# Graph convolution and masked attention on one core: small parameters loaded last, attention's first chunks reordered, the range check moved beside the last chunk

## The chip, the cores and the metric

The kernel runs on one core of a Trainium2 chip. The metric is the device time of one execution in microseconds (us), taken as the median of several runs; here it is 3640.62 us. The profile is of one execution, 3639.4 us from its first to its last instruction. Engines are named as the profile names them: PE is TensorE's matmul, PEld its weight load, DVE VectorE, ACT ScalarE, POOL GpSimd and SP SyncE, whose queue starts most transfers. A "q" behind a name (SPq, PEldq) is that engine's sequencer.

## What is computed

Two layers over x (8 batches of 2048 nodes with 256 features) and one adjacency matrix of 2048 x 2048, all in float32.

```python
# layer 0
A_norm = adj + eye;  dinv = rsqrt(rowsum(A_norm) + colsum(A_norm) - diag(A_norm))
agg = (A_norm * dinv[:, None] * dinv[None, :]) @ x            # for each batch
h = relu(batchnorm(agg @ W1.T + b1, g1, be1))                 # 512 wide
x = layernorm(x + batchnorm(h @ W2.T + b2, g2, be2))          # 256 wide
# layer 1: 4 heads of 64, mask where adj == 0
q, k, v = split(x @ W)
attn = softmax(q @ k.T / 8 + where(adj == 0, -inf, 0)) @ v
out = layernorm(x + attn)
```

The softmax is computed without subtracting the row's maximum. At the end a range check counts the row sums that lie outside 1e-20 to 1e30. If there is one, the whole attention is done again with maxima (`attention_with_maxima`, L1045); otherwise a branch jumps over that code.

## The kernel before, in words

**The load of the adjacency (L195 to L272).** Sixteen row tiles of 128 x 2048 (1 MB each, `a`, three buffers, L217) come in on SP's queue. For each tile PE makes sixteen transposes (L231, into PSUM tiles `ps`, four buffers), DVE and ACT copy them out (L237, L235), ACT sums the rows (L239), DVE takes the diagonal (L220), PE adds up the columns by a product with ones (L241, `pc`), and POOL prepares the mask's diagonal (L246, L247). The load of a further tile into a buffer waits until all of these have read it. In this block the order of SP, POOL and DVE is the order of the code; PE and ACT are ordered by the scheduler. Six small parameters are loaded at the very beginning, each with one transfer on SP's queue that scatters single floats to 128 partitions (L71): `b1s`, `g1s`, `be1s` (4 a partition) and `b2s`, `g2s`, `be2s` (2 a partition). They are first read by L366, by the first batch norm, by L557 and by the second batch norm. After the sixteenth tile come four loads of x (L251), the first weights (L252) and the writes of half of the transposed adjacency to DRAM, `bt_d`, four times 2 MB (L254).

**Layer 0 (L277 to L619).** Products of half-matrices on PE (`product`, L326: eight float32 matmuls of 512 columns into one of four PSUM tiles `pa`), with sums on DVE and POOL around them. Three difference tiles (`t2`, `t3`, `t4`) overwrite the quarters written out by L254, so each waits for one of these writes. The copy L390 waits for the last, because its tile lies in memory that the fourth quarter held.

**Attention's input and start (L989 to L1023).** The first batch has four chunks of 512 rows, numbered 0 to 3. For each chunk in turn: batch norm on ACT (`bn`), turned on PE and added to x on DVE in two halves (`turn_y`, `add_y`, through PSUM tile `st`), with the layer norm's statistics on DVE, and then its root on POOL (`root`). `ready(c)` applies the layer norm on ACT and, for chunks 0 and 1, turns the result on PE (`turn`, copied to `x1t` by ACT). `project` makes keys (1), queries (0) or values (2) of one chunk. The order here is written out by hand and kept on PE, DVE, ACT and POOL: all four chunks, `ready(0)`, three projections, `ready(1)`, the first scores.

**Attention (L1024 to L1043).** 64 units (batch, pair of heads, chunk of 512 queries), each of 16 steps, one for every 128 keys. A step computes scores on PE (L824), the mask on DVE (L836), the exponential on ACT (L842), the weighted sum of values on PE (L854) and the row-sum accumulator on POOL (L865). Scores run three steps ahead. Other work is hung onto steps by `at_step(unit, step, f)`; what is due after the last unit runs at the end, in order of its step. At the end of a unit: the sums are completed on PE (L881), copied by ACT (L889), turned on PE (L895), put into `sums_all` by DVE (L897); the outputs are turned (L908) and added to x (L916, 8 instructions, `finish` in two halves). For the second pair of heads follow the output's layer norm: `emit_stats` on DVE (L656, L658), `root` on POOL (L95, L97, L663, L664, four columns), `emit` on ACT (L668) and one 512 KB store on SP's queue (L749).

**The end (L1123 to L1141).** The range check runs after everything, in two pools of its own whose memory is reused: two instructions on DVE (L1130, L1131), one matmul (L1135), one conversion (L1136). Then each engine loads the count into a register (L1139) and branches (L1140).

Of the kernel before, what the change touches and what calls it, by code (L numbers as in the profile page):

```python
# [21 lines left out]
SUM_MIN = 1e-20  # L22
SUM_MAX = 1e30
# [3 lines left out]
def tile_gcn_then_masked_attention(  # L27
# [15 lines left out]
    nc = tc.nc  # L43
    ENG = mybir.EngineType
    PSUM = bass.MemoryType.PSUM
    P = 128
# [8 lines left out]
    CH = 512  # L55
    NCH = N // CH
# [9 lines left out]
    mhalf = cpool.tile([P, NT], F32, name="mhalf")  # L66
    nc.gpsimd.memset(mhalf, -0.5)

    def column_param(src, n, name):
        t = cpool.tile([P, n], F32, name=name)  # L70
        nc.sync.dma_start(t, src.rearrange("(c p) -> p c", p=P))  # L71
        return t

    b1s, g1s, be1s = (column_param(s, NH, n) for s, n in ((b1, "b1s"), (g1, "g1s"), (be1, "be1s")))
# [120 lines left out]
    with tc.tile_pool(name="bt7", bufs=1, side="right") as bp7, tc.tile_pool(  # L195
# [54 lines left out]
        for i, j in HALVES:  # L250
            S[0, i, j] = load_form(i, j, 0)  # L251
        nc.sync.dma_start(w1s, w1t.rearrange("(c p) f -> p c f", p=P))  # L252
        for s, ij in enumerate(HALVES):
            nc.sync.dma_start(bt_d[s], T[1, ij])  # L254
        cs = sp1.tile([P, CH], F32, name="cs")
# [385 lines left out]
    def rows(b, k, src, n=CH):  # L641
        return src[b, k * n : (k + 1) * n, :].rearrange("(t p) d -> p t d", p=P)

    class LayerNorm:
# [28 lines left out]
    class Layer1Input:  # L673
# [44 lines left out]
            self.ln[b, c].stats(tiles)  # L718

        def root(self, b, c):  # L720
            self.ln[b, c].root()

        def apply(self, b, c, half):
            self.ln[b, c].apply(range(IT * half, IT * (half + 1)))
# [16 lines left out]
        def emit_stats(self, b, c, half):  # L741
            if half == 0:
                self.ln[b, c] = LayerNorm(self.pool, self.x1[b, c])
            self.ln[b, c].stats(range(IT * half, IT * (half + 1)))

        def emit(self, b, c, half):
            self.apply(b, c, half)
# [43 lines left out]
                )  # L791

    IN_ORDER = {ENG.PE, ENG.DVE, ENG.Activation, ENG.Pool}

    def attention():


        with tc.tile_pool(
# [111 lines left out]
            def finish(u, half):  # L910
                b, hp, c = units[u]
                for i in range(IT * half, IT * (half + 1)):
                    t = inp.x1[b, c][:, i, :]
                    for h in range(2):
# [3 lines left out]
                            op0=ALU.mult, op1=ALU.add,  # L918
                        )

# [67 lines left out]

            with tc.manual_schedule(engines=IN_ORDER):  # L989
                for c in range(NCH):  # L990
                    inp.yt[0, c] = y0[c]
                    inp.x1[0, c] = ip.tile([P, TPC, D], F32, name="x1", bufs=NCH + 3)
                    for o in range(NO):
                        inp.bn(0, c, o)
                    pm = ps_s.tile([P, TPC, D], F32, name="st")
# [4 lines left out]
                    inp.root(0, c)  # L1000
                right.close()
# [4 lines left out]
                def ready(c):  # L1006
                    for half in range(2):
                        inp.apply(0, c, half)
                    if c < 2:
                        for half in range(2):  # L1010
                            inp.turn(0, c, half)

                ready(0)
                inp.project(0, 0, 0, 1, k_on_act=True)
                inp.project(0, 0, 0, 0)
                inp.project(0, 0, 0, 2)
                ready(1)
                for g in range(LEAD):
                    mask_scores(g, scores(g))
                    exps(g)  # L1020
                    if g == 1:
                        inp.project(0, 0, 1, 1)
                        ready(2)  # L1023
# [96 lines left out]
    attention()  # L1120


    with tc.tile_pool(name="range", bufs=1, space=PSUM) as ps_c, tc.tile_pool(  # L1123
        name="range_s", bufs=1
    ) as rp:
        flat = sums_all.rearrange("p u t h -> p (u t h)")
        ok = rp.tile([P, NU * TPC * 2], F32, name="ok")
        cnt = rp.tile([P, 1], F32, name="cnt")
        bad = cpool.tile([1, 1], mybir.dt.int32, name="bad")
        nc.vector.tensor_scalar(ok, flat, SUM_MIN, None, op0=ALU.is_ge)  # L1130
        nc.vector.scalar_tensor_tensor(  # L1131
            ok, flat, SUM_MAX, ok, op0=ALU.is_le, op1=ALU.mult, accum_out=cnt
        )
        pc = ps_c.tile([1, 1], F32, name="pc")
        nc.tensor.matmul(pc, cnt, ones[:, :1], start=True, stop=True)  # L1135
        nc.vector.tensor_scalar(  # L1136
            bad, pc, -1.0, float(P * NU * TPC * 2), op0=ALU.mult, op1=ALU.add
        )
        n_bad = nc.values_load(bad[0:1, 0:1])  # L1139
    with tc.If(n_bad > 0):  # L1140
        attention_with_maxima()  # L1141

# [42 lines left out]
```

## Time and profile before

| What | Value |
|---|---|
| Median of 3 runs | 3640.62 us (3638.4 to 3642.35) |
| Span of the profile | 3639.4 us, granted PE clock 0.993 |
| PE, POOL, DVE, ACT busy | 99%, 76%, 55%, 45% |
| Chain that ended last | PE 96%, POOL 1%, DVE 1%, ACT 1% |
| First PE instruction | 9.18 us |
| Layer 0's last product to the first scores | 1247.29 to 1282.19 us |
| Last value product (L854) to the end | about 3614.9 to 3639.4 us |

Busy shares are an average over very different stages. The kernel is PE's nearly everywhere; what PE does not fill are the head (before the first tile lands), the passage from layer 0 to attention, and the tail after the last value product. There the chain of waits and the timeline tell more than the shares do.

### The profile page before, as it was taken

The page shows a single profiled execution, that of the slowest core. Times are in us where ns is not written, and L with a number is a line of the kernel's source. Part 1 is how long each engine was busy: PE and PEld are TensorE (multiplying, and loading weights), DVE is VectorE, ACT ScalarE, POOL GpSimd, SP SyncE. Part 2 cuts the span into 40 slices and gives each one's busy share as a digit, 9 for nine tenths or more (in the row PEclk, how much of TensorE's full clock was granted, in tenths as well). Part 3 has the DMA queues.
Part 4 walks back from the last instruction along what each step waited for, and adds up shares of the span by engine and source line. Part 5 has one row for each costly group of instructions (what it writes and reads, how often), then busy time and mean ns, then how long its engine had stood idle before and what let it go on. Part 6 is the DMA issues. An engine that isn't in the chain of part 4 may idle for free.

```text
span 3639.4 us, 55807 instructions
## 1 busy us (share of the span) xinstructions
PE 3587.3 (99%) x23055; PEld 1487.6 (41%) x23055; DVE 1989.5 (55%) x2929; ACT 1642.6 (45%) x2036; POOL 2757.1 (76%) x1457
## 2 busy tenths in 40 slices
PE   8999999999999899999999999999999999999997
PEld 4444444444444443433343433343433334343332
DVE  6212141221146646766766766676676676676665
ACT  5001100110135455655665665565566566556554
POOL 3443263424247678999999999999999999999996
PEclk9999999999999899999999999999999999999998
DMA  9122232230256300000010010010001000000000
GB/s 338 61 75 87 81 133 81 75 98 29 81 204 252 147 1 7 24 30 13 19 42 13 13 36 24 13 36 24 7 30 36 7 24 30 13 19 24 7 1 25
DMA packets 132761, 205.82 MB, mean 57 GB/s; under 512 B 6912, under 2 KB 113936, under 8 KB 122000
## 3 DMA queue, kind: packets, MB, share of 16 engines
q1 hardware_dynamic: 132032, 196.11, 15.6%
q0 software_dynamic: 288, 4.98, 0.4%
q8 instruction: 183, 3.00, 0.3%
q10 hardware_dynamic: 176, 1.06, 0.1%
q14 instruction: 82, 0.67, 0.1%
HBM read 126.62 MB, written 75.51 MB: 56 GB/s over the span
## 4 chain that ended last, share of the span: by engine, by line
PE 96%; POOL 1%; DVE 1%; ACT 1%; DMA 0%; issue 0%; SPq 0%; POOLq 0%; DVEq 0%; ACTq 0%
PE out_ps L854 25%; PE st L824 24%; PE pa L329 21%; PE pm L765 6%; PE ph L362 5%; PE pa L539 5%; PE pm L779 3%; PE pm L881 2%; PE pm L707 1%; PE pm L733 1%; PE ps L231 1%; PE pm L908 1%; PE pm L895 1%; POOL acc L865 1%; PE ph L584 1%; PE pc L241 0%
## 5 line engine op out<-in xcount | busy, mean ns | idle before, releaser
L865 POOL TENSOR_TENSOR acc<-acc,prob 128x1024 f32<-128x1024 f32 x823 | 1947.5, 2366 | 97.8 <-ACT prob L842 40.6
L836 DVE SCALAR_TENSOR_TENSOR prob<-mask,st 128x1024 f32<-128x1024 uint8 x1024 | 1243.3, 1219 | 616.9 <-PE st L824 582.0
L842 ACT ACTIVATE prob<-prob 128x1024 f32<-128x1024 f32 x1024 | 1082.3, 1057 | 945.4 <-DVE prob L836 925.1
L854 PE MATMUL out_ps<-prob,v 64*64 64x512 f32 x8192 | 1077.1, 596 | 1.7 <-DVE ot L870 1.7
L824 PE MATMUL st<-qt,kt 64*64 64x512 f32 x8192 | 1064.2, 590 | 0.1
L329 PE MATMUL pa<-t,x 128*128 128x512 f32 x1792 | 773.2, 594 | 2.7 <-ACT x L305 2.7
L824 PEld LDWEIGHTS st<-qt,kt 64*64 64x64 f32 x8192 | 312.8, 133 | 566.9 <-issue 528.3
L329 PEld LDWEIGHTS pa<-t,x 128*128 128x128 f32 x1792 | 341.3, 191 | 432.6 <-issue 428.4
L854 PEld LDWEIGHTS out_ps<-prob,v 64*64 64x64 f32 x8192 | 284.9, 132 | 511.6 <-issue 412.7
L410 POOL TENSOR_TENSOR ag<-ag,dbc 128x512 f32<-128x512 f32 x16 | 20.2, 1262 | 486.1 <-DVE ag L409 456.6
L366 ACT ACTIVATE h<-ph,b1s 128x512 f32<-128x512 f32 x112 | 77.0, 688 | 404.4 <-PE ph L362 404.4
L765 PE MATMUL pm<-x1t,wq 128*128 128x512 f32 x512 | 247.2, 606 | 0.7 <-ACT x1t L739 0.7
L390 ACT COPY ag<-pa 128x512 f32<-128x512 f32 x16 | 9.4, 586 | 422.7 <-PE pa L329 411.6
L362 PE MATMUL ph<-ag,w1s 128*128 128x512 f32 x448 | 193.4, 592 | 0.0
L863 POOL TENSOR_TENSOR acc<-prob 128x1024 f32<-128x1024 f32 x64 | 151.2, 2362 | 32.5 <-ACT prob L842 31.0
L668 ACT ACTIVATE x<-x,ln_nm,ln_rs 128x256 f32<-128x256 f32 x256 | 137.4, 586 | 9.3 <-POOL ln_nm L664 9.3
L779 PEld LDWEIGHTS pm<-wq,x1t 128*128 128x128 f32 x1024 | 119.3, 192 | 29.3 <-issue 27.3
L367 DVE BATCH_NORM_STATS2 st<-h 128x6 f32<-128x512 f32 x112 | 76.9, 692 | 99.1 <-ACT h L366 99.1
L362 PEld LDWEIGHTS ph<-ag,w1s 128*128 128x128 f32 x448 | 85.1, 190 | 107.1 <-issue 106.9
L779 PE MATMUL pm<-wq,x1t 128*128 128x128 f32 x1024 | 128.4, 278 | 0.3 <-ACT x1t L739 0.3
L765 PEld LDWEIGHTS pm<-x1t,wq 128*128 128x128 f32 x512 | 88.2, 192 | 95.9 <-issue 89.1
L299 POOL TENSOR_TENSOR x<-x,dinv 128x1024 f32<-128x1024 f32 x60 | 116.7, 1966 | 0.0
(137 smaller groups left out, 2425.3 us busy)
## 6 DMA issues: line engine op xcount, KB each, us to landing
x<-in_x_dram SPq DMA_DIRECT2D x92, 512.0 KB, 4.1
h_d<-h SPq DMA_DIRECT2D x28, 1024.0 KB, 3.9
t<-h_d SPq DMA_DIRECT2D x28, 1024.0 KB, 7.9
a<-in_adj_dram SPq DMA_DIRECT2D x16, 1024.0 KB, 5.1
y_d<-ag SPq DMA_DIRECT2D x32, 512.0 KB, 2.7
out_dram<-x SPq DMA_DIRECT2D x32, 512.0 KB, 2.9
yt<-y_d SPq DMA_DIRECT2D x28, 512.0 KB, 3.2
bt_d<-t SPq DMA_DIRECT2D x4, 2048.0 KB, 16.1
```

Of the source, the lines that this page charges most:

```text
L329: nc.tensor.matmul(pa, s.t[:, m, :], t[:, m, :], start=(m == 0), stop=(m == HT - 1))
L362: nc.tensor.matmul(ph, w1s[:, d, f * P : (f + 1) * P], ag[:, d, :], start=(d == 0), stop=(d == ND - 1),)
L539: nc.tensor.matmul(py, w[:, f, :], t[:, f, :], start=(f == 0), stop=(f == 1))
L668: nc.scalar.activation(self.t[:, i, :], self.t[:, i, :], AF.Identity, bias=self.nm[:, i : i + 1], scale=self.rs[:, i : i + 1],)
L765: nc.tensor.matmul(pm, wq[:, d, wcols], xt[:, d, cols], start=(d == 0), stop=(d == ND - 1))
L779: nc.tensor.matmul(pm[:, j * P : (j + 1) * P], xt[:, d, t * P : (t + 1) * P], wq[:, d, wcols], start=(d == 0), stop=(d == ND - 1),)
L824: nc.tensor.matmul(st[r * HD : (r + 1) * HD, h, :], kt[hs, j * P + r * HD : j * P + (r + 1) * HD], qt[hs, cols], start=True, stop=True,)
L836: nc.vector.scalar_tensor_tensor(p, mask[:, j, cols][:, None, :].to_broadcast([P, 2, CH]), MASKED, st, op0=ALU.mult, op1=ALU.add,)
L842: nc.scalar.activation(probs[g], probs[g], AF.Exp)
L854: nc.tensor.matmul(outs[u][hs, r, :], inp.qkv[b, hp][2][rs, j, hs], probs[g][rs, h, :], start=(j == 0), stop=(j == NT - 1),)
L863: nc.gpsimd.tensor_add(accs[u], probs[g - 1], probs[g])
L865: nc.gpsimd.tensor_add(accs[u], accs[u], probs[g])
```

## The change

It does three things. The six parameter loads are collected and issued after the first weights, ahead of the writes to `bt_d`, so that the first adjacency tile can be requested at once. At attention's start only chunks 0 to 2 are made ready first; chunk 0 is turned and projected, and chunk 3 is turned and added behind those projections; chunk 1's layer norm is applied before them. At the end, the layer norm of the last chunk but one (unit 62) is moved up into the last unit's steps, the last chunk (unit 63) goes through statistics, root, apply and store in two halves of 256 rows (roots of two columns, stores of 256 KB), and the range check is done right behind the last statistics, in a tile of the attention's own pool.

In the built program two more instructions stand elsewhere, where the scheduler put them: a 512 KB load of x (L393's, into `x7`) is now fourth on SP's queue, behind the first three adjacency tiles, instead of behind the writes to `bt_d`; and PE takes the first tile's column sums (`pc`) ahead of its transposes.

```diff
+    params = []
     def column_param(src, n, name):
         t = cpool.tile([P, n], F32, name=name)
-        nc.sync.dma_start(t, src.rearrange("(c p) -> p c", p=P))
+        params.append((t, src.rearrange("(c p) -> p c", p=P)))
         return t
...
         nc.sync.dma_start(w1s, w1t.rearrange("(c p) f -> p c f", p=P))
+        for t, src in params:
+            nc.sync.dma_start(t, src)
         for s, ij in enumerate(HALVES):
             nc.sync.dma_start(bt_d[s], T[1, ij])
...
-        def root(self):
-            n = self.t.shape[1]
-            rsqrt(self.rs, self.mv[:, :, 1], n, EPS)
-            nc.gpsimd.tensor_scalar(self.nm, self.mv[:, :, 0], -1.0, None, op0=ALU.mult)
-            nc.gpsimd.tensor_mul(self.nm, self.nm, self.rs)
+        def root(self, tiles):
+            s = slice(tiles[0], tiles[-1] + 1)
+            rsqrt(self.rs[:, s], self.mv[:, s, 1], len(tiles), EPS)
+            nc.gpsimd.tensor_scalar(self.nm[:, s], self.mv[:, s, 0], -1.0, None, op0=ALU.mult)
+            nc.gpsimd.tensor_mul(self.nm[:, s], self.nm[:, s], self.rs[:, s])
...
+        def emit_half(self, b, c, half):
+            s = slice(IT * half, IT * (half + 1))
+            self.apply(b, c, half)
+            nc.sync.dma_start(rows(b, c, out)[:, s], self.x1[b, c][:, s])
...
+            def count_sums():
+                flat = sums_all.rearrange("p u t h -> p (u t h)")
+                ok = ap_.tile([P, CH], F32, name="ot")
+                cnt = ap_.tile([P, 1], F32, name="cnt", bufs=1)
+                nc.vector.tensor_scalar(ok, flat, SUM_MIN, None, op0=ALU.is_ge)
...
-                if hp == HP - 1:
+                if u == NU - 2:
+                    for half in range(2):
+                        at_step(u + 1, 8.3 + half, inp.emit_stats, b, c, half)
+                        at_step(u + 1, 13 + half, inp.emit, b, c, half)
+                    at_step(u + 1, 10.5, inp.root, b, c)
+                elif u == NU - 1:
+                    for half in range(2):
+                        at_step(u + 1, 6.3 + half, inp.emit_stats, b, c, half)
+                        at_step(u + 1, 6.4 + half, inp.root_half, b, c, half)
+                        at_step(u + 1, 8 + half, inp.emit_half, b, c, half)
+                    at_step(u + 1, 10, count_sums)
+                elif hp == HP - 1:
                     for half in range(2):
                         at_step(u + 1, 10.3 + 3 * half, inp.emit_stats, b, c, half)
                         at_step(u + 2, 3 + half, inp.emit, b, c, half)
...
+                for c in range(NCH - 1):
+                    ready(c)
+                halves(inp.apply, 0)
+                halves(inp.turn, 0)
+                halves(inp.apply, 1)
+                inp.project(0, 0, 0, 1, k_on_act=True)
+                inp.project(0, 0, 0, 0)
+                ready(NCH - 1)
                 right.close()
...
-                ready(0)
-                inp.project(0, 0, 0, 1, k_on_act=True)
-                inp.project(0, 0, 0, 0)
                 inp.project(0, 0, 0, 2)
-                ready(1)
+                halves(inp.turn, 1)
```

In the changed kernel `ready(c)` stands for turning chunk c, adding it to x and taking its root; `halves(f, c)` calls f for both halves of a chunk. The old block of the range check behind `attention()` is removed but for the load of the count and the branch.

More of the change, by code (lines that the diff above doesn't have):

```diff
@@ L720, in root, with root_half @@
         def root(self, b, c):
-            self.ln[b, c].root()
+            self.ln[b, c].root(range(TPC))
+        def root_half(self, b, c, half):
+            self.ln[b, c].root(range(IT * half, IT * (half + 1)))
         def apply(self, b, c, half):
@@ L793, in tile_gcn_then_masked_attention @@
     IN_ORDER = {ENG.PE, ENG.DVE, ENG.Activation, ENG.Pool}
+    bad = cpool.tile([1, 1], mybir.dt.int32, name="bad")
     def attention():
@@ L919, in finish @@
                         )
+            def count_sums():
[3 more added lines that the diff above has]
+                nc.vector.tensor_scalar(ok, flat, SUM_MIN, None, op0=ALU.is_ge)
+                nc.vector.scalar_tensor_tensor(
+                    ok, flat, SUM_MAX, ok, op0=ALU.is_le, op1=ALU.mult, accum_out=cnt
+                )
+                pm = ps_m.tile([1, 1], F32, name="pm")
+                nc.tensor.matmul(pm, cnt, ones[:, :1], start=True, stop=True)
+                nc.vector.tensor_scalar(
+                    bad, pm, -1.0, float(P * NU * TPC * 2), op0=ALU.mult, op1=ALU.add
+                )
             LEAD = 3
@@ L994, in attention, with ready @@
                         inp.bn(0, c, o)
+                def ready(c):
                     pm = ps_s.tile([P, TPC, D], F32, name="st")
@@ L1000, in attention, with halves @@
                     inp.root(0, c)
+                def halves(f, c):
+                    for half in range(2):
+                        f(0, c, half)
+                for c in range(NCH - 1):
[6 more added lines that the diff above has]
+                ready(NCH - 1)
                 right.close()
@@ L1004, in attention @@
                 )
[L1006 to L1011, printed above, removed]
-                ready(0)
-                inp.project(0, 0, 0, 1, k_on_act=True)
-                inp.project(0, 0, 0, 0)
                 inp.project(0, 0, 0, 2)
-                ready(1)
+                halves(inp.turn, 1)
                 for g in range(LEAD):
@@ L1022, in attention @@
                         inp.project(0, 0, 1, 1)
-                        ready(2)
+                        halves(inp.apply, 2)
                 for g in range(NU * NT):
@@ L1120, in tile_gcn_then_masked_attention @@
     attention()
[L1123 to L1139, printed above, removed]
+    n_bad = nc.values_load(bad[0:1, 0:1])
     with tc.If(n_bad > 0):
```

## The prediction

> **What bounds the kernel now.** The page's chain gives PE 96% of the span, so time can come only from stretches where PE waits. I read the chain of waits in order of time over three: the head, layer 0 to attention, and the tail. The head, from the chain (start, us, what):
>
> ```profile
> 3.37 0.47 SPq L71
> 3.83 0.04 issue
> 3.88 5.20 DMA a<-in_adj_dram
> 9.07 0.14 issue
> ```
>
> Six parameter issues fill SP's queue from 0.73 us, and the first tile, asked for at 3.88, lands at 9.07. From there to 59.4 the chain is PE but for one transfer at 37.42, which costs PE 0.41 us (its idle total behind `a` is 9.6 over two waits, the longest 9.2). But DMA is nearly as full. The table by stretches (the last columns are PE clock, DMA share, GB/s) shows the only slack, about 2 us, behind the third tile:
>
> ```profile
> 10.00:15.00 5.00, 5.00 (x33) 3.83 (x32) 3.04 (x6) 4.43 (x6) 1.00 (x2) 1.00 0.73 287
> 15.00:20.00 5.00, 5.00 (x41) 2.69 (x39) 3.69 (x10) 2.65 (x5) 1.97 (x4) 1.00 0.86 316
> 20.00:25.00 5.00, 5.00 (x44) 3.63 (x47) 3.65 (x8) 4.19 (x6) 0.98 (x2) 1.00 0.97 347
> ```
>
> Attention's start, again from the chain: the four chunks pass one by one between PE and DVE, then chunk 0 is turned, projected, and PE waits for ACT to apply chunk 1's norm.
>
> ```profile
> 1265.57 0.70 DVE x L715
> ...
> 1269.02 1.72 PE pm L733 x8
> ...
> 1271.40 5.89 PE pm L765 x8
> ...
> 1279.59 2.08 ACT x L668 x4
> ```
>
> The tail, from the timeline: two norms on POOL and ACT, the store, and only after it has landed the check.
>
> ```profile
> 3618.35 0.35 ACT L889 COPY sm<-pm 128x256 f32<-128x256 f32 x1
> ...
> 3627.26 0.37 SPq L749 DMA_DIRECT2D out_dram<-x  x1
> 3630.78 0.43 DVE L1130 TENSOR_SCALAR ok<-sums_all 128x512 f32<-128x512 f32 x1 [7.67 <-DMA out_dram<-x]
> ...
> 3632.38 0.14 DVE L1136 TENSOR_SCALAR bad<-pc 1x1 int32<-1x1 f32 x1 [0.43 <-PE pc L1135]
> ```
>
> Behind that lies the branch, from the view of line 1140:
>
> ```profile
> L1140 SPq EVENT_SEMAPHORE  x8: 17/17/17, 3636.5 to 3637.0; - x8
> ...
> L1140 PEldq COMPARE_BRANCH  x1: 4465/4465/4465, 3633.2 to 3633.2; - x1
> ```
>
> **What the Trainium skill says.** "TensorE: Matmul & The Clock Gate", Part 1: after an idle window of about 3.4 us PE runs at half rate, until it has been busy for one. The trace agrees: over attention's start the granted clock is 0.50 to about 1275.9, 1.00 to about 1282.7, 0.50 again to about 1286. "Runtime: NRT & Kernel Launch", Instruction fetch mechanics: a taken branch out of the loaded window waits for its target to be fetched. That fits the 4.465 us on PE and the 3.2 to 3.6 us from branch to next record elsewhere. "DMA: Bandwidth & Descriptors", Rules for kernel authors: a last dimension that is not contiguous becomes one descriptor per element. 2264 packets, all under 512 B, in the first 5 us agree. The same page, Anatomy of one DMA (written for POOL's transfers): about 2 us fixed plus bytes. Here 2 KB lands in 2.2 us, the last 512 KB store in 2.93.
>
> **The change, part by part.** Times are on the clock of before.
>
> *Head.* Taken off SP's queue: six issues of 0.43 to 0.51 us, 0.73 to 3.88, so 3.15 us; the landing (5.20) I leave alone but for 0.05. POOL's `ident` is ready at 1.45 and does not bind. 3.2 us.
> The x load (512 KB) moves in behind the third tile. At 250 to 420 GB/s it needs 1.3 to 2.1 us of DMA. The fourth tile is asked for when the first is released, at 13.9 (10.75 shifted), and its data cannot start for about 2 us; that is the hole above. It lands about 5 us after its issue, and PE wants it three tiles after the first, at 19.93 (16.8 shifted): a margin of 1 us. Cost 0, hidden in the hole; upper bound 1.5.
> `pc` first on PE: the same work, four products of 1.0 us in all, moved ahead of sixteen transposes that run slow now (3.65 against 1.9 us), which I put down to the cold clock, though the record has it at 1.00 there. What is slow changes, not how long. DVE's copies start some 1 to 2 us later for one tile; DVE needs about 2.4 of each 2.89 us and catches up. 0.
> The parameters at their new place: six issues of 0.5 us (3 us), more if the queue is full (x issues there take up to 3 us, one 17.8). Behind them on SP are the four `bt_d` writes, the mask's, and the next x loads. Now the first `bt_d` goes out at 59.2 after SP waited for POOL's last addition (L247, to 58.8), while the weights' issue ends at 59.1, so all 3 us count, and up to 8 as a bound. Who waits: L390, until 83.38, for the last `bt_d` write. It frees the PSUM tile of the first product, which PE needs after four products of 6.87 us, at 92.6: slack 8.6. `t2` starts at 73.74, the first write lands at 68.7; the sum it feeds is due at 85.8, ready at 78.2: slack 7.6. POOL's chain through the broadcast dinv (95.44) has POOL's scaled x ready at about 98.5 for a product at 113, and the sum for the next unit's second product at 107 for 120. 3 us, and 7 too, lie beside PE's products. 0.
>
> *Attention's start.* In the chain chunk 2's last transposes end at 1265.55, chunk 3's at 1269.02. Chunk 0's turn moves up by 3.47 us. Behind it: turn 1.72, copy 0.65, two projections 5.9 (mostly cold), then new on PE's way chunk 3: two groups of transposes of 0.5 us with DVE's addition between them, 0.76 including its two hand-overs, 1.8 in all; values 1.85; chunk 1's turn 1.0 without waits, its norm having been applied meanwhile. Sum 12.9 to 13.1, against 13.25 now from 1269.02 to 1282.27. So scores start 3.47 + 0.2 = 3.7 us earlier. Also the gaps before 1282 go, which had let the clock fall: scores and projection took 5.44 where full rate gives 3.44; ACT and the mask on DVE keep about 1.2 of these 2. Whether the clock stays up depends on where the windows fall, an even chance, so I take 0.5. 4.2 us, bounds 2 and 5.5.
> In front of the mask DVE has chunk 3's additions and statistics, some 3.5 us beginning during the projections' end, done about when the first scores are. Attention then is PE-bound, and passes the shift on.
>
> *Tail.* (a) Unit 62's norm. POOL's root (1.96 us) moves ahead of its last two additions; the accumulator is ready at 16.3 instead of 14.3 past 3600, and PE's ones product on it starts at 16.58: just hidden. ACT's four applies (2.07) move ahead of the copy of `ot`; the sums' copy no longer waits for them, 17.2 instead of 18.35. Unit 62's statistics at steps 8 and 9 push masks back by up to 1.3 us, of which 0.2 reaches PE's last products. Gain 0.9.
> (b) The halves. After the sums: 4 additions 0.82, statistics 0.87; root of two columns 1.6 (the power took 0.57 for one column, 1.04 for four; taken 0.73 for two); apply 1.04. The second half's DVE work (1.69) is as long as the first root, so POOL goes on at once: store at about 3625.0 instead of 3627.26, of which 0.9 is (a). SP's extra store, 0.37, lies beside the second root. 256 KB should land in 2.6, at 3627.6.
> (c) The check. Its 1.74 us now runs behind DVE's last statistics (3622.25), done at 3624.0, beside root and apply. DVE's next is only the load of the count. PE loads and branches from 3624.05: now 3632.6 to 3637.65 is 5.05, so 3629.1. SP branches behind its last store: loads at 3625.4, then 3.9 to its semaphore waits and 0.5 for these: 3629.8. Last store landed before that. From the end of these waits to the end of the kernel is 1.7 us: 3631.5. Against 3639.4 the tail gives 7.9 us, with (a) and (b) in it; bounds 6 and 8.8.
>
> Sum: 3.2 + 4.2 + 7.9 = 15.3, so 3640.6 - 15.3 = 3625.3 us.
>
> **The rivals.**
> *DMA takes the head's gain back* (15%). The x load's 1024 descriptors hold up the fourth tile by 1.5 us, or the late `bt_d` outlasts its slack. For it: DMA share 0.97 and more from 20 us on, 17.8 us for one issue. Against it: the hole and slacks of 7 to 8 us. Gain 0 there: 3628.5.
> *Attention starts PE no sooner* (15%). Chunk 3's additions hold DVE when the first mask is due, or the clock falls in another window (3.4 us at half rate is 1.7). Gain 1.5 instead of 4.2: 3628.0.
> *The tail's end is set by another wait* (9%). Branches at different times on five engines take longer to fetch, or the accumulator comes late on PE. Gain 4: 3629.2.
> *Slower* (3%). The parameters' scattered 4-byte writes crawl behind a full queue and hold `bt_d` by some 30 us: 30 - 8.6 = 21 us on PE in layer 0, 15 back: 3646.6. Against it: at the start of the kernel they land in 2.2 to 2.7 us each.
>
> **How the numbers follow.** The forecast has 58%. The single rivals end near 3628 to 3629; two together near 3631 to 3632. If all goes well (3.3, 5.5, 8.8) it is 3623, and runs differ by 2 us either way. Range 3620.5 to 3632.5. A change of 0.2% is 7.3 us, the line is 3633.3; only three rivals together or the slow case lie beyond. Faster 0.92, same 0.05, slower 0.03.
>
> **What would show it.** First PE work at about 6.0 us and no new wait for `a` at the fourth tile; L390's wait longer, but PE's products in layer 0 without a gap; scores 7 us earlier than 1282.2 (3.2 of it from the head), the clock not falling behind them; the sums' copy about 0.9 us sooner after the last value product; the check done before the last store; about 6.5 us from that store to the end where it is 12.1 now. The prediction is wrong if PE waits in layer 0 for L390 or POOL, if the branch costs more than now, or if attention's first units give the shift back.

## The result and the profile after

The changed kernel takes 3625.11 us, the median of 4 runs (3622.15 to 3625.88), against 3641.3 us for the kernel before (4 runs, 3638.4 to 3642.35). The ratio is 0.9955, with a 95% interval of 0.9938 to 0.9973. The profiles' spans are 3624.1 and 3639.4 us. The forecast was 3625.3. By the medians that is 16.2 us less, by the two traces 15.3.

The three parts of the change lie far apart in time, and between the first copy of a unit's row sums (`sm`) in attention and the last unit's products with ones, which complete its row sums on PE, nothing moved (2269.0 and 2268.9 us). So the span can be split by four marks that every trace has:

| Stretch | before | after | saved | forecast |
|---|---|---|---|---|
| start to the last batch norm's first `bn_aggr` (layer 0's end) | 1250.09 | 1247.37 | 2.72 | 3.2 |
| from there to the first sums' copy (attention's start) | 95.77 | 90.96 | 4.81 | 4.2 |
| from there to the start of PE's last products with ones | 2268.97 | 2268.92 | 0.05 | 0 |
| from there to the end | 24.57 | 16.85 | 7.72 | 7.9 |
| sum | 3639.4 | 3624.1 | 15.3 | 15.3 |

**The head.** The chain of waits of the changed kernel in order of time (start, length, what) now begins with the first tile itself:

```profile
0.73 4.79 DMA a<-in_adj_dram
...
5.66 1.93 PE pc L243 x8
7.59 5.12 PE ps L233 x32
...
16.70 5.88 DMA a<-in_adj_dram
...
34.43 5.84 DMA a<-in_adj_dram
```

The tile is asked for at 0.73 instead of 3.88, lands in 4.79 instead of 5.20, and PE starts at 5.66 instead of 9.21: 3.55 us. Twice after that the chain goes through a transfer, where it was once before. The table by stretches (time on PE, PEld, DVE, ACT, POOL, then PE clock, DMA share, GB/s) shows that the hole behind the third tile is filled:

```profile
10.00:15.00 5.00, 5.00 (x42) 3.99 (x41) 4.08 (x11) 3.04 (x5) 2.00 (x4) 1.00 0.95 292
...
20.00:25.00 5.00, 4.67 (x41) 3.19 (x43) 3.80 (x8) 3.92 (x6) 1.10 (x2) 1.00 0.97 362
```

DMA is at 0.95 from 10 us on, where it had 0.73, and PE misses 0.33 us between 20 and 25, waiting for the sixth tile.

**Attention's start**, from the chain of the changed kernel:

```profile
1261.70 1.12 PE st L711 x4
1262.81 1.72 PE pm L740 x8
...
1265.19 6.12 PE pm L777 x8
1271.32 0.45 PE st L711 x4
...
1275.66 0.66 PE pm L740 x4
1276.31 1.06 PE st L838 x8
```

Chunk 0 is turned (L740) right behind chunk 2's transposes. The fourth chunk (L711 at 1271.32) stands behind the two projections (L777). Chunk 1's turn (L740 at 1275.66) no longer waits for ACT's 2.08 us of L668. Scores (L838) start at 1276.31 instead of 1282.27.

**The tail**, from the timeline of the changed kernel (start, length, engine, line; in brackets the idle time before and what ended it):

```profile
3609.68 0.37 ACT L903 COPY sm<-pm 128x256 f32<-128x256 f32 x1 [1.07 <-PE pm L895]
...
3612.93 0.23 POOL L97 TENSOR_SCALAR ln_rs<-ln_mv 128x2 f32<-128x2 f32 x1 [4.29 <-DVE ln_mv L662]
...
3614.37 0.46 POOL L668 TENSOR_TENSOR ln_nm<-ln_nm,ln_rs 128x2 f32<-128x2 f32 x1
3614.38 0.39 DVE L940 TENSOR_SCALAR ot<-sums_all 128x512 f32<-128x512 f32 x1
3614.80 0.69 DVE L941 SCALAR_TENSOR_TENSOR ot<-sums_all,ot 128x512 f32<-128x512 f32 x1
...
3614.91 0.68 POOL L97 TENSOR_SCALAR ln_rs<-ln_mv 128x2 f32<-128x2 f32 x1
...
3615.88 0.15 DVE L946 TENSOR_SCALAR bad<-pm 1x1 int32<-1x1 f32 x1 [0.37 <-PE pm L945]
3615.97 2.53 SPq L756 DMA_DIRECT2D out_dram<-x  x2
...
3616.79 0.20 POOL L668 TENSOR_TENSOR ln_nm<-ln_nm,ln_rs 128x2 f32<-128x2 f32 x1
```

The count (L946) is done at 3616.03, just as the first of the two stores (L756) is being issued; the second goes out at 3618.13. The view of the branch's line, one engine a row:

```profile
L1168 SPq EVENT_SEMAPHORE  x8: 17/17/17, 3621.7 to 3622.2; - x8
L1168 PEldq COMPARE_BRANCH  x1: 3805/3805/3805, 3616.7 to 3616.7; - x1
...
L1168 SPq COMPARE_BRANCH  x1: 45/45/45, 3619.1 to 3619.1; - x1
```

PE's branch comes 2.4 us ahead of SP's, since it does not stand behind the issue of a store. SP's is the last, and its semaphore records (3621.7 to 3622.2) lead to the end at 3624.1.

### The profile page after: what moved, and what is told of

It is laid out like the page before. It is cut to its first block, busy times and chain, and to the rows that moved or that the text cites. A ratio compares the mean times of both kernels' runs of the same rounds, so it can differ in the third digit from the quotient of the medians.

```text
span 3624.1 us, 55802 instructions
## 1 busy us (share of the span) xinstructions
PE 3585.2 (99%) x23055; PEld 1486.7 (41%) x23055; DVE 1988.9 (55%) x2929; ACT 1642.7 (45%) x2036; POOL 2761.0 (76%) x1461
## 4 chain that ended last, share of the span: by engine, by line
PE 97%; DVE 1%; DMA 0%; ACT 0%; POOL 0%; issue 0%; POOLq 0%; ACTq 0%; SPq 0%; DVEq 0%
PE out_ps L868 25%; PE st L838 24%; PE pa L333 21%; PE pm L777 6%; PE ph L366 5%; PE pa L543 5%; PE pm L791 3%; PE pm L895 2%; PE pm L711 1%; PE pm L740 1%; PE pm L922 1%; PE ps L233 1%; PE pm L909 1%; PE ph L588 1%; DMA a<-in_adj_dram 0%; PE pc L243 0%
## 5 line engine op out<-in xcount | busy, mean ns | idle before, releaser
L838 PE MATMUL st<-qt,kt 64*64 64x512 f32 x8192 | 1062.9, 589 | 0.1
L838 PEld LDWEIGHTS st<-qt,kt 64*64 64x64 f32 x8192 | 312.6, 133 | 566.5 <-issue 527.0
L777 PE MATMUL pm<-x1t,wq 128*128 128x512 f32 x512 | 247.1, 606 | 0.7 <-ACT x1t L746 0.7
L394 ACT COPY ag<-pa 128x512 f32<-128x512 f32 x16 | 9.4, 586 | 423.1 <-PE pa L333 409.6
L877 POOL TENSOR_TENSOR acc<-prob 128x1024 f32<-128x1024 f32 x64 | 151.3, 2364 | 20.4 <-ACT prob L856 19.2
L777 PEld LDWEIGHTS pm<-x1t,wq 128*128 128x128 f32 x512 | 88.1, 192 | 95.1 <-issue 88.3
```

What stands on the lines that cost most here:

```text
L777: nc.tensor.matmul(pm, wq[:, d, wcols], xt[:, d, cols], start=(d == 0), stop=(d == ND - 1))
L838: nc.tensor.matmul(st[r * HD : (r + 1) * HD, h, :], kt[hs, j * P + r * HD : j * P + (r + 1) * HD], qt[hs, cols], start=True, stop=True,)
L877: nc.gpsimd.tensor_add(accs[u], probs[g - 1], probs[g])
```

## The experiments

Single traces differ by some 2 us at layer 0's end, and over attention's start by up to 3.8 us for the same code, as experiment 3 shows. So each part is judged by three things: its timed median against the kernel before, run beside it (medians of 3640.8 to 3641.2 us), its interval, and its own stretch in the trace.

**1. The head alone.** The kernel before, with the six parameter loads behind `w1s` (and the two moves of the scheduler that follow).

```diff
-        nc.sync.dma_start(t, src.rearrange("(c p) -> p c", p=P))
+        params.append((t, src.rearrange("(c p) -> p c", p=P)))
...
+        for t, src in params:
+            nc.sync.dma_start(t, src)
```

> Only the parameter loads are moved (the scheduler moves the x load and the column sums with them). Theory: the head alone gives what the changed kernel's trace shows at layer 0's end, 2.7 us (3.55 at the first product, of which 0.4 goes again over the sixteen tiles and 0.4 in the first product of layer 0): about 3638 us. Rival: the head's shift also moves the clock's windows at attention's start and the gain is 1 to 5 us, depending on where they fall.

Measured: 3636.66 us, ratio 0.9988 (0.9982 to 0.9995), so 4.6 us (1.8 to 6.5 by the interval, which holds both expectations). In its trace PE starts at 5.80, layer 0 ends 3.9 us sooner, and attention's start takes 95.8 us as before; so the rival, a gain by moved windows of the clock, doesn't show in it. The head's gain is real, and the forecast's 3.2 lies within the interval. The 2.72 us of the first pair of traces is at the low end of the scatter.

**2. Attention's start alone.** The kernel before with the new order of chunks.

```diff
+                for c in range(NCH - 1):
+                    ready(c)
+                halves(inp.apply, 0)
+                halves(inp.turn, 0)
+                halves(inp.apply, 1)
+                inp.project(0, 0, 0, 1, k_on_act=True)
+                inp.project(0, 0, 0, 0)
+                ready(NCH - 1)
...
-                ready(0)
-                inp.project(0, 0, 0, 1, k_on_act=True)
-                inp.project(0, 0, 0, 0)
                 inp.project(0, 0, 0, 2)
-                ready(1)
+                halves(inp.turn, 1)
...
```

> Only attention's start is reordered. Theory: scores start 3.2 us earlier, and some 1.6 us more come from the clock, which no longer falls behind them: 4.9 us, 3636 us. Rival: without the head's shift the windows of the clock fall differently, and 3.2 us or less is left: 3637.5 us.

Measured: 3636.4 us, ratio 0.9988 (0.9981 to 0.9995), 4.8 us. From layer 0's end to the first sums' copy it takes 91.34 us, against 95.77: the scores start 2.9 us sooner, and 1.6 us more come behind them, where the clock did not fall.

**3. The tail alone.** The kernel before with units 62 and 63 and the check as in the changed kernel.

```diff
+                if u == NU - 2:
...
+                    at_step(u + 1, 10.5, inp.root, b, c)
+                elif u == NU - 1:
...
+                        at_step(u + 1, 6.4 + half, inp.root_half, b, c, half)
+                        at_step(u + 1, 8 + half, inp.emit_half, b, c, half)
+                    at_step(u + 1, 10, count_sums)
```

> Only the tail is changed. Theory: 24.5 us from the end of the last value product to the end of the kernel become 16.8: 7.7 us less, 3633 us. Rival: part of this came from the two other parts, and 5 to 6 us are left.

Measured: 3632.92 us, ratio 0.9976 (0.9967 to 0.9985), 8.3 us. The tail is 17.2 us long instead of 24.57. This run showed something else by accident. Its code at attention's start is that of the kernel before, and yet that stretch took 92.00 us instead of 95.77, because the two projections took 3.70 us instead of 5.89 and the clock didn't fall at the first scores. (The run with this trace, 3630.15 us, is one of three low ones among its twelve; the other nine took 3632.1 to 3633.7.) The three singles add up to 17.7 us, against 16.2 for the whole, within what their intervals leave.

**4. The check alone.** The kernel before, with one whole last chunk and one 512 KB store, but the check run behind the last chunk's statistics.

```diff
+                if u == NU - 1:
+                    at_step(u + 1, 13.35, count_sums)
...
```

> Only the range check is moved behind the last statistics; unit 62's norm and the whole last chunk stay as before. Theory: the store is still issued about 12.4 us after the last value product, and from there the end is about 6 us away as in the changed kernel, instead of 12.1: 6 us less, 3634.5 us, so the check is most of the tail. Rival: the branch's fetch stays as long as before and starts after the store, 6.8 us: 5 us less. If the halves and unit 62 were the larger part, it would be under 4.

Measured: 3636.07 us, ratio 0.9986 (0.9979 to 0.9993), 5.2 us. In its trace the tail gives only 3.9 us, and two things in it make it less than 6. POOL's root was slowed by the check on DVE: the power took 1.45 us instead of 1.04, and the store went out 0.5 us later after PE's last products with ones.

```profile
3623.84 1.45 POOL L97 TENSOR_TENSOR ln_rs<-ln_rs,mhalf 128x4 f32<-128x4 f32 x1
```

And from SP's branch to its next records it took longer than before, from 3629.0 to 3633.4:

```profile
L1151 SPq EVENT_SEMAPHORE  x8: 17/17/17, 3633.4 to 3633.9; - x8
...
L1151 SPq COMPARE_BRANCH  x1: 45/45/45, 3629.0 to 3629.0; - x1
```

That is 4.4 us, against 2.5 in the changed kernel and 3.4 before. The theory that the check's place alone is worth 6 us does not hold in this trace (the interval of the times, 2.5 to 7.6 us, would allow it). A new one, that the fetch of the branch's target is held up by the 512 KB store just issued, went into experiment 5.

**5. The last chunk whole.** The changed kernel, but unit 63 with one root of four columns and one store, and the check still behind the last statistics.

```diff
-                        at_step(u + 1, 6.3 + half, inp.emit_stats, b, c, half)
-                        at_step(u + 1, 6.4 + half, inp.root_half, b, c, half)
-                        at_step(u + 1, 8 + half, inp.emit_half, b, c, half)
-                    at_step(u + 1, 10, count_sums)
+                        at_step(u + 1, 7.3 + half, inp.emit_stats, b, c, half)
+                        at_step(u + 1, 9 + half, inp.emit, b, c, half)
+                    at_step(u + 1, 8.5, inp.root, b, c)
+                    at_step(u + 1, 10.5, count_sums)
```

> The changed kernel, but the last chunk goes whole: one root of four columns, one store of 512 KB, and the check behind its last statistics. The halves were priced at 1.4 us. Theory: SP's branch after a store of 512 KB takes longer to fetch its target than after one of 256 KB (4.4 us in the run with the check alone, 2.6 in the changed kernel)[...]; then this kernel loses 1.4 for the store, about 0.5 for POOL slowed down by the check and 1.5 to 1.8 for the fetch: 3.2 to 3.7 us, about 3628.6, with 4 us or more from SP's branch to its semaphore records. Rival: the 4.4 us had to do with something else in that run; then the loss is 1.4 to 1.9 us, about 3626.8, with 2.6 to 3 us there.

Measured: 3627.46 us (5 runs, 3624.74 to 3627.62), 2.35 us slower than the changed kernel by the medians. The runs of the two overlap, so the reading rests on the tail of its trace: 19.2 us instead of 16.85. The total lies between the two expectations. The branch is as the theory had it:

```profile
L1168 SPq EVENT_SEMAPHORE  x8: 17/17/17, 3623.3 to 3623.8; - x8
...
L1168 SPq COMPARE_BRANCH  x1: 45/45/45, 3618.9 to 3618.9; - x1
```

From the branch to the next records it takes 4.3 to 4.4 us again. Both kernels with a 512 KB store issued right ahead of the branch need that, and the seven traced with the halves (this change, the tail alone, and experiments 6, 7, 8, 10 and 11) need 2.5 to 3.0. So the two go together; that the fetch itself is held up is not shown. The packets in these two traces speak against a fetch that still runs: for the last 1.5 us and more before SP's records (3621.6 to 3623.3 here, 3631.9 to 3633.4 in experiment 4) no DMA queue moves anything, those for instructions included. The store landed 3.8 us after its issue in both (2.9 before, 2.6 to 2.9 for the second half), and the records follow its landing by 1.5 and 1.6 us (0.6 to 1.3 with the halves). A wait that hangs on the landing is a rival that no run here separates.

The store itself is issued only 1.0 us later (11.87 instead of 10.88 us after the start of PE's last products with ones), where 1.4 and 0.5 were expected. So the halves gain in two ways in this pair of traces: 1.0 us in the store, and 1.8 from the branch to the next records, less 0.4 in the last records.

**6. Unit 62's norm at its old place.** The changed kernel without that move.

```diff
-                if u == NU - 2:
-                    for half in range(2):
-                        at_step(u + 1, 8.3 + half, inp.emit_stats, b, c, half)
-                        at_step(u + 1, 13 + half, inp.emit, b, c, half)
-                    at_step(u + 1, 10.5, inp.root, b, c)
-                elif u == NU - 1:
+                if u == NU - 1:
```

> The changed kernel with the norm of unit 62's chunk at its old steps, two units later. The prediction priced its early place at 0.9 us, all of it in the wait of the sums' copy on ACT for unit 62's four applies. If that is right, the copy comes 0.9 to 1.1 us later after PE's last value product, and so does the end: 3626.1. If PE's products of the ones on POOL's accumulator, which the early norm makes later, cost as much as that, there is no difference or this one is faster.

Measured: 3625.67 us (5 runs, 3625.25 to 3627.12), 0.56 slower; that alone can't be told from no difference. In the trace the sums' copy comes 3.51 us after PE's last products with ones begin, instead of 2.43, and the tail is 18.18 us long instead of 16.85. So the 0.9 us was 1.1.

**7. The early load of x.** The changed kernel, with the x tile made late by one written element, so that its load stands behind the last adjacency tile as before.

```diff
+        if late:
+            nc.gpsimd.tensor_copy(f.t[:, 0, 0:1], dinv[:, 0:1])
...
-                S[w, 0, 0] = load_form(nb, 0, nd)
+                S[w, 0, 0] = load_form(nb, 0, nd, late=first)
```

> The changed kernel, with one part of the head undone: the first load of x (512 KB) waits until POOL has written one element of its tile behind the last adjacency tile, so that it is asked for where the kernel before asked for it; the parameters stay late. The prediction took the load's early place as free: then no difference (within 0.3 us), and the fourth adjacency tile comes no earlier. The rival: the early load takes DMA time from the adjacency tiles, and this kernel is 0.4 to 1.5 us faster than the changed one, with shorter waits of PE for a tile between 10 and 55 us.

Measured: 3624.93 us (5 runs, 3622.78 to 3626.56), 0.2 us from the changed kernel. DMA's share from 10 to 15 us falls back to 0.61, and PE's two waits for a tile come at the same places (16.51 and 34.16) and cost 0.5 us in all instead of 0.6. The load fits the hole; no cost of it can be seen. The other move of the scheduler, `pc` ahead of the transposes, was not undone alone.

**8. The parameters three times.** The changed kernel with each parameter loaded three times, so that SP reaches `bt_d` later.

```diff
-        for t, src in params:
-            nc.sync.dma_start(t, src)
+        for _ in range(3):
+            for t, src in params:
+                nc.sync.dma_start(t, src)
```

> The changed kernel, with each of the six parameters loaded three times into the same tile, so SP's queue is held about 10 us longer (twelve issues of 0.5 to 1.1 us) in front of the four writes of the second half of the adjacency. The prediction gave these writes a slack of 7 to 8 us, of which the change took 5 as measured on SP. If the slack is as stated, the first write comes 10 us later, and PE waits in layer 0 for 3 to 4 us: 3 us slower than the changed kernel. If PE does not depend on these writes at all in this range, no difference; if the slack were used up already, 10 us slower.

Measured: 3625.66 us (5 runs, 3623.56 to 3627.49), no difference from the changed kernel, where 3 us were expected. The twelve added issues took 0.4 to 0.5 us each, so `bt_d` went out 5.8 us later and not 10. DVE now waits for it:

```profile
DVE t L342 <- DMA bt_d<-t: 3.4, 1, 3.4
```

(line waited for, us in total, times, longest). The copy that frees the first product's tile ends 30.6 us after that product's start. It was 21.8 in the kernel before and 24.3 in the changed one, and PE needs the tile after 30.4 (four products, 9.8 and three times 6.87). PE's matmuls run on without a gap, and its weight loads waited 1.0 us once. So the slack of 8.6 us was as stated, and this run used it up without overdrawing it.

**9. Each half of attention's new order alone.** First chunk 1's norm applied ahead of the projections, with the fourth chunk left early; then the fourth chunk late, with the norm of chunk 1 left where it was. Both are edits of the kernel before.

```diff
-                    if c < 2:
+                    if c == 0:
                         for half in range(2):
                             inp.turn(0, c, half)
                 ready(0)
+                ready(1)
...
-                ready(1)
+                for half in range(2):
+                    inp.turn(0, 1, half)
```

> Before, with one edit: the layer norm of chunk 1 is applied before chunk 0 is projected, so that ACT has done it long before PE turns chunk 1; the fourth chunk stays ahead of the projections, as it was. The whole middle took off 4.8 us. If most of it comes from the fourth chunk's place, as the prediction had it (3.5 of 4.2), this kernel gains 1.5 us or less. If the applied norm carries a part of its own, it takes away the two gaps of PE in front of chunk 1's turn (together about 2.2 us) and with them the fall of PE's clock behind them (1.6 us): 3.8 us, and PEclk stays at full rate between 1280 and 1290 us.

The second:

```diff
+                for c in range(NCH - 1):
+                    ready(c)
+                halves(inp.apply, 0)
+                halves(inp.turn, 0)
...
+                ready(NCH - 1)
...
-                ready(1)
+                halves(inp.apply, 1)
+                halves(inp.turn, 1)
```

> Before, with the other edit of the middle alone: the fourth chunk is turned and added behind the first two projections; the norm of chunk 1 is applied where it was. The prediction's working gives 3.5 us for the start of chunk 0's turn less 1.8 for the fourth chunk's transposes on PE's way: 1.7 us. The other reading, that the place of the fourth chunk is the whole gain, gives 4 to 5 us. With 1.7 the two gaps in front of chunk 1's turn are still there in the trace, and the clock falls behind them as before.

Measured: 3638.62 us (ratio 0.9992, 0.9985 to 0.9998) and 3638.31 us (0.9994, 0.9988 to 1.0001), so 2.6 and 2.9 us by the medians; the second interval just reaches no difference, and the traces tell more. The chain with the norm early:

```profile
1269.42 1.72 PE pm L733 x8
...
1271.80 3.70 PE pm L765 x8
...
1277.96 0.66 PE pm L733 x4
1278.62 1.06 PE st L824 x8
```

and with the fourth chunk late:

```profile
1265.62 1.72 PE pm L733 x8
...
1278.07 2.08 ACT x L668 x4
...
1280.74 1.06 PE st L824 x8
```

The early norm shortens the way from the values' end to the scores from 3.19 to 1.32 us: 1.9, where the two gaps had been put at 2.2. The late fourth chunk starts chunk 0's turn 3.5 us sooner and the scores 1.6 us sooner (both from layer 0's end): the 1.7 of the working. But here the clock did not fall behind the gap, though it had been expected to. In both traces the stretch from the first scores to the first sums' copy is 62.0 us, against 63.6 in the kernel before. So the working by instructions holds for both edits, and the 1.6 us of the clock cannot be assigned to either. The projections' 3.70 us in the first are the clock as well: PE's work ahead of them is unchanged.

**10. PE kept busy.** All these differences of 2 to 4 us led to the question whether PE's slow products are the clock's doing. The changed kernel got products that nothing reads, where PE stands idle.

```diff
+        for _ in range(18):
+            nc.tensor.matmul(pw, ones, ones, start=True, stop=True)
...
+        for _ in range(6):
+            nc.tensor.matmul(pw, ident, cs, start=True, stop=True)
...
+                        nc.tensor.matmul(pw[:, 0, :], ident, wq[:, 0, :CH], start=True, stop=True)
```

> The changed kernel with products that nothing reads, put where PE stands idle: 18 on ones before the first adjacency tile (about 3.5 us), 6 in front of layer 0's first product (2.6 us at full rate), 12 between layer 0 and attention's first turn (5.2 us) and 4 before each of the chunks 1 and 2 there (1.7 us each). If the slow first products after a gap are the clock's doing, the first sixteen transposes fall from 3.65 to about 1.9 us (of which the DMA behind may give back most), the first product of layer 0 from 10.2 to about 7 us, chunk 0's turn from 1.72 to about 0.95 and the two projections behind it from 6.1 to about 3.6: 6 to 7 us sooner at attention's scores, about 3619. If they are slow for another reason (operands just written, the first use of a buffer), the durations stay and the filling costs 0 to 5 us. In between, if the clock doesn't hold through the chunks' half-filled gaps: about 3 us gained in layer 0 and none in attention.

Measured: 3626.0 us (5 runs, 3625.32 to 3626.43), no gain. But the durations fell as the theory of the clock says. Layer 0's first product (L343) took 6.87 us instead of 10.19, chunk 0's turn (L750) 0.45 for its first half where both halves had taken 1.72, and the projections (L787) 3.70 instead of 6.12:

```profile
60.70 6.87 PE pa L343 x16
...
1244.81 10.30 PE out_ps L1064 x24
...
1265.60 0.45 PE pm L750 x4
...
1267.20 3.70 PE pm L787 x8
```

The filling itself (L1064) ate the gain: twelve products are 24 instructions and took 10.30 us, where 5.2 had been reckoned, because a float32 product of 128 x 512 is two instructions of 0.43. (In this kernel and the next, the x load is back behind the tiles; experiment 7 found no cost in its place.)

**11. Half the filling.** 11, 3, 6 and 3 products in place of 18, 6, 12 and 4.

> The kernel with the unread products again, each place filled with about half as many, since one product of 128x512 took 0.86 us at full rate (two instructions of 0.43) where 0.43 was reckoned: 11 ahead of the first tile, 3 in front of layer 0's first product, 6 in front of attention's first chunk, 3 at the chunks 1 and 2. If the clock explains the slow products, and the fuller version only paid its gain back in filling, then layer 0's first product starts at about 58.5 us and takes 6.9; attention's first turn comes about 4.5 us sooner after layer 0 than with the fuller filling, and the projections behind it keep 3.7 us: about 7 us sooner than that version, 3619, which is 6 us faster than the changed kernel. If half the filling is too little to keep the clock, the first product goes back to 9.8 to 10.2 us or the projections to 6, and 2 to 3 us of gain are left, 3622 to 3623.

Measured: 3619.66 us, 5 runs from 3619.03 to 3621.5, ratio to the kernel before 0.9944 (0.993 to 0.9957). All five lie below the lowest of the changed kernel's runs (3622.15), so it is the fastest on record; the intervals of the two ratios overlap, and the two were not timed side by side. Its trace is 6.9 us shorter than the changed kernel's:

```profile
1260.76 3.70 PE pm L787 x8
...
1269.46 1.06 PE st L848 x8
```

Layer 0 ends 2.8 us sooner: its first product takes 6.9 us, but the second then waits 0.96 us for ACT, which has not scaled its input yet. Attention's start gives 4.1 us more. The tail is unchanged (16.85 us).

## Why the prediction was right

**The sum and its parts.** Because of the scatter by the clock, the best comparison is over all traces that have a part and all that lack it (experiments 10 and 11 left out):

| Part | forecast | first pair | mean over all traces |
|---|---|---|---|
| head, at layer 0's end | 3.2 | 2.72 | 3.2 (6 with, 6 without) |
| attention's start | 4.2 | 4.81 | 3.9 (6 with, 4 without) |
| tail | 7.9 | 7.72 | 7.4 (4 with, 5 without) |

The three parts were right in their kind and nearly in their size. That the first pair of traces adds up to 15.3 to the tenth is luck: misses of -0.5, +0.6 and -0.2 us cancel in it, and the runs of the changed kernel alone lie 3.7 us apart.

**The head.** Right in its mechanism and nearly in its sum. The landing gave 0.41 us where 0.05 was put, and the same trace gave 0.83 back. Of this 0.43 went over the sixteen tiles: PE waits twice for a tile (0.33 and 0.29 us, once and 0.41 before), and the slow start stretches `pc` to 1.93 us and the transposes behind it, where "What is slow changes, not how long" had been priced at 0. Another 0.40 went in layer 0's first product, 10.19 us instead of 9.79. The x load at no visible cost is experiment 7's result. The parameters' issue was undersized: 5.0 us and not 3, single ones up to 1.15 behind the loads of x and of the weights. It did not matter, because the slack of 7 to 8.6 us was there (experiment 8): the wait of L394 (L390 before) grew from 11.1 to 13.5 us and PE had no gap.

**Attention's start.** The 3.47 us for chunk 0's turn came out as 3.49. From there to the scores it took 13.5 us, where 12.9 to 13.1 was worked out: the projections were slow for 6.12 us instead of 5.89, and from chunk 3's last transposes to the scores it took 3.1 us instead of 2.85, with chunk 1's turn waiting in its middle for ACT to copy the values. So the scores came 3.24 us sooner and not 3.7, and 6.0 with the head's part, where 7 was named. The term for the clock was undersized in this pair, 0.5 against 1.57; over all traces, one of which had the faster windows with the old code, the whole stretch gave 3.9, close to the 4.2. That the gaps before 1282 "had let the clock fall" is not shown: in experiment 3 and in the second kernel of experiment 9 the gap in front of chunk 1's turn is still there, and the clock stays at 1.00 behind it. It fell behind the first scores in three of four traces with the old order and in none of six with the new one (experiments 10 and 11 left out). That slow products are the clock's doing is shown by experiments 10 and 11: with PE kept busy the granted clock stays at 1.00 and the durations fall to those of full rate. This agrees with the Trainium skill, "TensorE: Matmul & The Clock Gate", Part 1, which also says that the window runs freely and does not begin with the kernel. That fits the scatter here: the same code took 92.0 and 95.8 us.

**The tail.** (a) 0.9 us for unit 62 was 1.1. (b) The second store was to go out 10.17 us after PE's last products with ones and went out at 10.88. The step that failed is the check of which it was said "Its 1.74 us now runs behind DVE's last statistics (3622.25), done at 3624.0, beside root and apply", at no cost to them. While DVE ran L940 and L941, POOL's L668 took 0.46 us instead of 0.20 and L97 0.68 instead of 0.23: 0.71 in all, as much as the whole difference. In experiment 4 the same check slowed the four-column power. The Trainium skill, "SBUF — State Buffer", Who interferes with whom, says that DVE and POOL share one pair of ports under an exclusive lock, and that a DVE instruction with two inputs in SBUF contends with a POOL one that reads SBUF. The trace agrees: L97 started 0.11 us into L941, which has two, and ended 0.1 us after it. L668 was slower beside L940, which has one input; that sentence does not cover it, and no run here tells why. The power on two columns was estimated at 0.73 us and took 0.73 and 0.72. (c) SP's branch as the last one was right, and PE's (3.8 us, from 3616.7) is hidden. From SP's load to its semaphores it took 3.1 us instead of 3.9, and from their end to the kernel's end 1.9 instead of 1.7; this gave back most of what POOL lost.

**The rivals.** None came. DMA did not hold `bt_d` beyond its slack, attention did start sooner, the accumulator stayed hidden (PE's product on it was followed at once by the sums' copy at 3609.68), and the parameters landed without a pile-up (2.3 to 5.2 us after their issue, against 2.2 to 2.7).

## What to carry to other kernels

Price the parts of a change stretch by stretch between marks that both traces have; then a sum that is right because its misses cancel is seen as such, and so is noise in one stretch. Here gaps of PE cost more than their length: products behind them ran at half rate for several us, and filling the gaps with unread products, sized by their real duration, was worth some 5 us more by the medians (3619.66 against 3625.11, not timed side by side). Work put "beside" another engine is not free for that alone: the check cost POOL's roots 0.71 us. Ask what the neighbour does on the critical path in that very microsecond.

## What the runs showed of the hardware that was not expected

- The time from a taken branch to the next record on SP differed with what was just put on the DMA queue: 2.5 to 3.0 us behind a 256 KB store (seven traces), 4.4 behind one of 512 KB (two traces), and 3.4 in the kernel before (3.2 to 3.5 in five traces with its tail), where no store was in flight but all five engines branched within 0.1 us. Why is open.
- The range check on DVE (1.1 us) slowed two-column instructions on POOL by 0.26 and 0.45 us, and a four-column power from 1.04 to 1.45 us (1.46 in experiment 5).
- Attention's start, with the same code, took 92.0 us in one trace and 95.7 to 95.8 in three; the same instructions ran faster, with the clock on record higher. In the two traces with some 19 and 29 us of unread products the granted clock is 0.999 and 0.998 over the whole span, against 0.993 to 0.996 in the twelve others.
- Loading a parameter of 2 KB or less cost SP 0.43 to 0.51 us for each issue at the start of the kernel before, and 0.47 to 1.15 us behind the loads of x and of the weights.
